# Graph attention with residual norms: running sums in place, keys and values per half of the heads, and a new order of the fill-in work

## The chip, the cores and the metric

The kernel runs on one core of one Trainium2 chip. The metric is the device time of one execution in microseconds (us), the median of several runs. Five engines of the core work side by side, each on its own list of instructions: TensorE (PE in the profile; its weight loads are listed as PEld) multiplies matrices into PSUM, VectorE (DVE) and ScalarE (ACT) compute on SBUF and PSUM, GpSimd (POOL) computes on SBUF, and SyncE (SP) starts DMA transfers. GpSimd starts those DMAs that add to their destination. An engine takes its instructions in the order in which the program gave them to it.

## The reference: what is computed

Eight graphs of 2048 nodes with 256 channels share one adjacency matrix. One layer of masked attention with 8 heads of 32 channels is followed by two normalisations and a small MLP, and the result is added to the input and normalised once more. Cut to what matters:

```python
# x: (8, 2048, 256) float32, adj: (2048, 2048) int32
q, k, v = split(einsum('fnc,ck->fnk', x, w_qkv), 3)         # 8 heads of 32
scores = einsum('fnhd,fmhd->fhnm', q, k) / sqrt(32)
scores = where(adj > 0, scores, -1e9)
t = einsum('fhnm,fmhd->fnhd', softmax(scores), v)
y = layernorm(x + t) * ln1_g + ln1_b
h = relu(y @ w1 + b1)
z = layernorm(y + h @ w2 + b2) * ln2_g + ln2_b
out = layernorm(x + z)
```

## The kernel before

For each graph `f` the nodes are cut into 4 query chunks of 512 (`qc`) and 16 key blocks of 128 (`mb`), and the heads into 2 halves of four (`g`). One **item** is (f, qc, g, mb); there are 8 x 4 x 2 x 16 = 1024 of them, and 16 consecutive items with the same (f, qc, g) are called a **group** here, so a graph is 8 groups. The main loop makes one item after the other:

```python
def scores(item):                       # PE: 4 matmuls, DVE: 2 adds of the mask, ACT: 1 exp
    pt = PT[item] = pp.tile([P, 4, CH], F32, name="p")
    ps2 = [score_pair() for _ in range(2)]          # 2 of 3 pairs of PSUM banks
    for half in (1, 0):
        for j in range(2):
            r = D * (2 * half + j)
            nc.tensor.matmul(ps2[half][:, j, :], KT[f, mb // TPC][r:r + D, g, ...], QT[f, qc][r:r + D, g, :], ...)
    for half, ps in enumerate(ps2):
        nc.vector.tensor_tensor(pt[:, 2 * half:2 * half + 2, :], ps, MK[f, qc][:, mb, None, :]..., ALU.add)
    nc.scalar.activation(pt, pt, AF.Exp, scale=1.0 / math.sqrt(D))

def values(item):                       # PE: 4 matmuls into the group's output bank
    for h in range(4):
        nc.tensor.matmul(O[grp][r:r + D, :], V[f, mb // TPC][:, mb % TPC, ...], PT[item][:, h, :], ...)

def add_up(item):                       # sums of the 16 exp tiles, for the denominators
    for chain in CHAINS:                # ((2, 5, 8, 11), (3, 6, 10, 13)): a DMA adds to the first one
        if mb in chain[1:]:
            nc.gpsimd.dma_start(PT[f, qc, g, chain[0]], PT.pop(item), accum_op=ALU.add)
    if mb == POOLED[1]:                 # POOLED = (0, 1, 4, 7, 9, 12, 14): GpSimd adds into "acc"
        ACC[grp] = ap.tile([P, 4, CH], F32, name="acc")
        nc.gpsimd.tensor_tensor(ACC[grp], PT.pop((f, qc, g, POOLED[0])), PT.pop(item), ALU.add)
    elif mb in POOLED[2:]:
        nc.gpsimd.tensor_tensor(ACC[grp], ACC[grp], PT.pop(item), ALU.add)
```

All other work is cut into steps by generators. A `yield n` means "go on no sooner than n items from now". One bank of PSUM is left for this fill-in work while a group runs; `bank()` hands it out. The generators are `denominator` (per group: 16 matmuls of the sums with ones, then 4 transposes), `tail` (per query chunk: everything after the attention), `project` (per chunk of 512 nodes: queries, keys and values of the next graph), and in the first graph `turn_mask` (the transposed mask, kept in DRAM for the later graphs).

```python
def project(f, c):
    xc = ld.tile(...); nc.sync.dma_start(xc, x[f, c * CH:(c + 1) * CH, :]...)
    yield 3
    while state["turned"]: yield 0
    state["turned"] = True              # one tile "turned" for project and tail
    for a in range(2):                  # 4 transposes, a copy by ACT; yield 1
        ...
    for store, pool, name, k0 in ((KT, kp, "kT", C), (QT, qp, "qT", 0)):
        for g in range(2):              # 2 matmuls of 512 columns, a copy by ACT; yield 1
            ...
    for jj in range(0, TPC, 2):         # V: 4 matmuls of 256 columns, a copy by ACT; yield 1
        for j in range(jj, jj + 2):
            for a in range(2):
                nc.tensor.matmul(ps[...], xT[:, a, j * P:(j + 1) * P], wqkv[:, a, 2 * C:], ...)
    V[f, c] = dst; state["turned"] = False; yield 1

def tail(f, qc):
    while state["y"]: yield 0           # the tail of the chunk before must have ended
    state["y"] = True
    # 2 x (4 transposes, DVE multiplies by 1/denominator); yield 1 each
    nc.gpsimd.dma_start(y, xin, accum_op=ALU.add)       # y += x
    yield 4
    yield from norm(y)                  # DVE statistics of 4 tiles; yield 1; POOL; yield 2; ACT; yield 1
    # 2 x 4 transposes (into "turned"), 2 x 2 matmuls with w1, 2 x 4 matmuls with w2, each with a yield 1
    yield from norm(z)
    nc.gpsimd.dma_start(z, xin, accum_op=ALU.add)       # z += x
    yield 5
    yield from norm(z)
    nc.sync.dma_start(out[...], z); state["y"] = False
```

The main loop (`advance` runs one step of the first generator in the list that is due; `denominator` and `tail` are put at the head of the list):

```python
for t, (f, qc, g, mb) in enumerate(items):
    # ... group starts: load_mask, mask_ahead ...
    if f + 1 < F and qc == NCK - 1:     # the next graph's projections: in the last two groups
        if g == 0 and mb == 0: start(t, projections(f + 1, 0, 1))
        if g == 1 and mb % TPC == 0 and mb: start(t, projections(f + 1, mb // TPC, mb // TPC + 1))
    if mb:
        advance(t)
        if mb % 2: advance(t)
    if t + LEAD < len(items):           # LEAD = 2
        while (nf, nmb // TPC) not in V:            # not projected yet: do it now
            advance(t0); t0 += 1
        scores(items[t + LEAD])
    values(items[t])
    add_up(items[t])
    if mb == LAST: start(t + SUM, denominator(f, qc, g), urgent=True)      # SUM = 4
```

`KT`, `QT` and `V` have 5 tiles each: four chunks of one graph and one more. Before the loop, the constants are loaded by DMAs that SyncE starts, and the first graph is projected.

Of the kernel before, what the change touches and what calls it, by code (L numbers as in the profile page):

```python
# [10 lines left out]
F32 = mybir.dt.float32  # L11
# [16 lines left out]
SUM_MAX = 1e19  # L28

# [23 lines left out]
def fast_path(ctx, tc, cst, x, adj, out, RS):  # L53
# [7 lines left out]
    kp = ctx.enter_context(tc.tile_pool(name="kp", bufs=NCK + 1))  # L61
    qp = ctx.enter_context(tc.tile_pool(name="qp", bufs=NCK + 1))
    vp = ctx.enter_context(tc.tile_pool(name="vp", bufs=NCK + 1))
    pp = ctx.enter_context(tc.tile_pool(name="pp", bufs=9))
    ap = ctx.enter_context(tc.tile_pool(name="ap", bufs=1))
# [11 lines left out]
    state = {"pair": 0, "side": None, "turn": 0, "turned": False, "y": False}  # L77
# [20 lines left out]
    def turn_mask(qc, mc):  # L98
        if mc == 0:
            MK[0, qc] = mkp.tile([P, MB, CH], F8, name="mask")  # L100
        cv = ld.tile([P, TPC, CH], BF16, name="in")
        for half in range(2):
            t = ld.tile([P, 2, CH], I32, name="in")
            q0 = qc * CH + half * 2 * P
            nc.sync.dma_start(t, adj[q0:q0 + 2 * P, mc * CH:(mc + 1) * CH].rearrange("(j p) m -> p j m", p=P))
            nc.vector.tensor_scalar(cv[:, 2 * half:2 * half + 2, :], t, 0.0, MASKED, op0=ALU.is_le, op1=ALU.mult)
            yield 1
        yield 1
        for half in range(2):
            ps = bank(BF16)  # L110
            for r in range(2):
                for j in range(TPC):
                    rr = 2 * half + r
                    nc.tensor.transpose(ps[:, r, j * P:(j + 1) * P], cv[:, j, rr * P:(rr + 1) * P], identb)
            nc.scalar.copy(MK[0, qc][:, mc * TPC + 2 * half:mc * TPC + 2 * half + 2, :], ps, saturate=False)
            yield 1
        if mc == NCK - 1:
            nc.sync.dma_start(MD[qc], MK[0, qc])
# [8 lines left out]
    def project(f, c):  # L127
        xc = ld.tile([P, TPC, C], F32, name="in")
        nc.sync.dma_start(xc, x[f, c * CH:(c + 1) * CH, :].rearrange("(j p) c -> p j c", p=P))
        yield 3  # L130
        while state["turned"]:
            yield 0
        state["turned"] = True
        xT = work.tile([P, 2, CH], F32, name="turned")
        for a in range(2):
            ps = bank()
            for j in range(TPC):
                nc.tensor.transpose(ps[:, j * P:(j + 1) * P], xc[:, j, a * P:(a + 1) * P], ident)
            nc.scalar.copy(xT[:, a, :], ps)
            yield 1  # L140
        for store, pool, name, k0 in ((KT, kp, "kT", C), (QT, qp, "qT", 0)):
            dst = pool.tile([P, 2, CH], F32, name=name)
            for g in range(2):
                ps = bank()
                for a in range(2):
                    nc.tensor.matmul(ps, wqkv[:, a, k0 + g * P:k0 + (g + 1) * P], xT[:, a, :],  # L146
                                     start=(a == 0), stop=(a == 1))
                nc.scalar.copy(dst[:, g, :], ps)  # L148
                if g == 0:
                    yield 1  # L150
            store[f, c] = dst
            yield 1
        dst = vp.tile([P, TPC, C], F32, name="v")
        for jj in range(0, TPC, 2):
            ps = bank()
            for j in range(jj, jj + 2):
                for a in range(2):
                    nc.tensor.matmul(ps[:, (j - jj) * C:(j - jj + 1) * C], xT[:, a, j * P:(j + 1) * P],  # L158
                                     wqkv[:, a, 2 * C:], start=(a == 0), stop=(a == 1))
            nc.scalar.copy(dst[:, jj:jj + 2, :], ps.rearrange("p (b c) -> p b c", c=C))  # L160
            if jj == 0:
                yield 1
        V[f, c] = dst
        state["turned"] = False
        yield 1


    PT, O, OT, DT, ACC, RC = {}, {}, {}, {}, {}, {}

    def scores(item):  # L170
        f, qc, g, mb = item
        pt = PT[item] = pp.tile([P, 4, CH], F32, name="p")
        ps2 = [score_pair() for _ in range(2)]

        for half in (1, 0):
            for j in range(2):
                r = D * (2 * half + j)
                nc.tensor.matmul(ps2[half][:, j, :], KT[f, mb // TPC][r:r + D, g, (mb % TPC) * P:(mb % TPC + 1) * P],  # L178
                                 QT[f, qc][r:r + D, g, :], start=True, stop=True)
        for half, ps in enumerate(ps2):  # L180
            nc.vector.tensor_tensor(pt[:, 2 * half:2 * half + 2, :], ps,  # L181
                                    MK[f, qc][:, mb, None, :].to_broadcast([P, 2, CH]), ALU.add)
        nc.scalar.activation(pt, pt, AF.Exp, scale=1.0 / math.sqrt(D))  # L183
# [3 lines left out]
    def values(item):  # L187
        f, qc, g, mb = item
        grp = (f, qc, g)
        if mb == 0:  # L190
            i = state["side"]
            O[grp] = ps_x[i].tile([P, CH], F32, name=f"x{i}")
        for h in range(4):
            r = D * h
            nc.tensor.matmul(O[grp][r:r + D, :], V[f, mb // TPC][:, mb % TPC, g * P + r:g * P + r + D], PT[item][:, h, :],  # L195
                             start=(mb == 0), stop=(mb == LAST))
        if mb == LAST:
            OT[grp] = op.tile([P, CH], F32, name=f"oT{g}")
            nc.scalar.copy(OT[grp], O.pop(grp))
# [3 lines left out]
    POOLED = (0, 1, 4, 7, 9, 12, 14)  # L203
    CHAINS = ((2, 5, 8, 11), (3, 6, 10, 13))
    SUM = 4

    def add_up(item):
        f, qc, g, mb = item
        grp = (f, qc, g)
        for chain in CHAINS:  # L210
            if mb in chain[1:]:
                nc.gpsimd.dma_start(PT[f, qc, g, chain[0]], PT.pop(item), accum_op=ALU.add)  # L212
        if mb == POOLED[1]:
            ACC[grp] = ap.tile([P, 4, CH], F32, name="acc")
            nc.gpsimd.tensor_tensor(ACC[grp], PT.pop((f, qc, g, POOLED[0])), PT.pop(item), ALU.add)  # L215
        elif mb in POOLED[2:]:
            nc.gpsimd.tensor_tensor(ACC[grp], ACC[grp], PT.pop(item), ALU.add)  # L217


    def norm(t):  # L220
# [5 lines left out]
        yield 1  # L226
# [14 lines left out]
    def denominator(f, qc, g):  # L241
        grp = (f, qc, g)
        terms = [PT.pop((f, qc, g, LAST))] + [PT.pop((f, qc, g, chain[0])) for chain in CHAINS] + [ACC.pop(grp)]
# [7 lines left out]
        yield 1  # L251
        ps = bank()
# [12 lines left out]
    def tail(f, qc):  # L265
        while state["y"]:
            yield 0
        state["y"] = True
# [3 lines left out]
        for gg in range(2):  # L272
            oT = OT.pop((f, qc, gg))
            ps = bank()
# [5 lines left out]
            yield 1  # L280
        nc.gpsimd.dma_start(y, xin, accum_op=ALU.add)
        yield 4
        yield from norm(y)
        while state["turned"]:
            yield 0
        state["turned"] = True
        yT = work.tile([P, 2, CH], F32, name="turned")
        for a in range(2):
            ps = bank()
# [3 lines left out]
            yield 1  # L293
# [3 lines left out]
        for d in range(2):  # L297
            ps = bank()
# [3 lines left out]
            yield 1  # L302
        state["turned"] = False
        z = y
        for jj in range(0, TPC, 2):
            ps = bank()
# [5 lines left out]
            yield 1  # L312
# [4 lines left out]
        yield 5  # L317
        yield from norm(z)
        nc.sync.dma_start(out[f, qc * CH:(qc + 1) * CH, :].rearrange("(j p) c -> p j c", p=P), z)
        state["y"] = False  # L320
# [4 lines left out]
    def start(t, gen, urgent=False):  # L325
        fill.insert(0 if urgent else len(fill), [t, gen])

    def run(e, t):
        wait = next(e[1], None)
        if wait is None:  # L330
            fill.remove(e)
        else:
            e[0] = t + wait
        return wait != 0

    def advance(t):
        for e in list(fill):
            if e[0] <= t and run(e, t):
                return
# [5 lines left out]
    def projections(f, c0, c1):  # L345
        for c in range(c0, c1):
            yield from project(f, c)

    items = [(f, qc, g, mb) for f in range(F) for qc in range(NCK) for g in range(2) for mb in range(MB)]
    LEAD = 2  # L350
    for c in range(NCK):
# [7 lines left out]
    for t, (f, qc, g, mb) in enumerate(items):  # L359
# [6 lines left out]
        if f + 1 < F and qc == NCK - 1:  # L366
            if g == 0 and mb == 0:
                start(t, projections(f + 1, 0, 1))
            if g == 1 and mb % TPC == 0 and mb:
                start(t, projections(f + 1, mb // TPC, mb // TPC + 1))  # L370
        if mb:
            advance(t)
            if mb % 2:
                advance(t)
        if t + LEAD < len(items):
            nf, _, _, nmb = items[t + LEAD]
            t0 = t
            while (nf, nmb // TPC) not in V:
                advance(t0)
                t0 += 1  # L380
# [6 lines left out]
    while fill:  # L387
        t += 1
        advance(t)
# [125 lines left out]
def kernel(  # L515
# [23 lines left out]
    def weight(name, src):  # L539
        t = cst[name] = const.tile([P, 2, src.shape[1]], F32, name=name)  # L540
        nc.sync.dma_start(t, src.rearrange("(a p) k -> p a k", p=P))

    def row_of(pool, name, v):
        t = cst[name] = pool.tile([P, C], F32, name=name)
        nc.sync.dma_start(t, bass.AP(tensor=v.tensor, offset=v.offset, ap=[[0, P], [1, C]]))

    def cols_of(name, v):
        t = cst[name] = const.tile([P, 2], F32, name=name)
        nc.sync.dma_start(t, v.rearrange("(a p) -> p a", p=P))
# [76 lines left out]
```

## Time and profile before

| | value |
|---|---|
| median of 3 runs | 4095.39 us (4093.89 to 4095.95) |
| span of the profiled execution | 4091.3 us |
| first item's mask add starts at | 70.8 us |
| last item's mask add starts at | 4009.6 us |
| mean granted TensorE clock | 0.947 |
| VectorE, ScalarE, GpSimd busy | 67%, 60%, 64% of the span |
| DMA: queue of GpSimd, queue of SyncE | 53.4%, 6.6% of 16 engines' span |

In the profile a line such as `L181 DVE TENSOR_TENSOR p<-s,mask ... x2048 | 2410.5, 1219 | 968.3 <-PE s L178 827.2` reads: source line 181, on VectorE, writes a tile p from s and mask, 2048 times; together 2410.5 us busy, 1219 ns each; the engine stood idle for 968.3 us just before these instructions, 827.2 us of it until the matmuls of line 178 had written s. In the timeline a line begins with the start and the length of a run of equal instructions, and the bracket at its end tells how long the engine had been idle and what ended that. The table of stretches gives, for each stretch of the span, its length, then the busy time of each engine with the number of instructions, the mean granted clock and the share of the DMA engines.

The number of items per group is always 16, so 16 times the shortest distance between items is what a group could take; the distances themselves are read from the starts of the mask adds of line 181, two for each item.

### The profile page before, as it was taken

The numbers are of one execution on the slowest core, as the hardware profiler recorded it, in microseconds if no ns is written. First come the engines' busy times: TensorE is split into PE (matmuls) and PEld (weight loads), VectorE is DVE, ScalarE is ACT, GpSimd is POOL, SyncE is SP. The second block draws the span as 40 slices with busy tenths as digits, with TensorE's granted clock in tenths as the row PEclk, the third lists the DMA queues.
The fourth block names the chain that finished last, engine by engine and source line by source line (L and its number), as shares of the span: only waits on it lengthen the run. The fifth ranks groups of instructions, "written<-read, shape, count | busy, mean of one in ns | idle before, by whom it ended". The sixth has DMA issues, their size and how long they took to land. (4 is left out here: it accounts for less than half of the span.)

```text
span 4091.3 us, 52692 instructions
## 1 busy us (share of the span) xinstructions
PE 3308.0 (81%) x21508; PEld 1011.5 (25%) x21508; DVE 2745.5 (67%) x3175; ACT 2443.2 (60%) x1953; POOL 2624.4 (64%) x1355
## 2 busy tenths in 40 slices
PE   7777788878887888888878878877888878888883
PEld 3222132212222222222222222222222222222221
DVE  3777756777567774777647776477755777567772
ACT  4565555666566664666647666466655666556662
POOL 1576655776567774777747776477754777557774
PEclk9899899999999999999999999999999999999996
DMA  4766745666556664567746667376654677546663
GB/s 122 160 139 150 175 97 105 137 134 147 109 108 144 144 138 99 109 134 152 153 94 130 127 132 150 83 150 145 131 115 99 136 148 157 110 101 135 134 130 74
DMA packets 138792, 525.52 MB, mean 128 GB/s; under 512 B 10160, under 2 KB 76848, under 8 KB 85296
## 3 DMA queue, kind: packets, MB, share of 16 engines
q0 software_dynamic: 89088, 436.24, 53.4%
q1 hardware_dynamic: 49456, 85.86, 6.6%
q8 instruction: 170, 2.79, 0.3%
q14 instruction: 78, 0.64, 0.0%
HBM read 98.44 MB, written 20.97 MB: 29 GB/s over the span
## 5 line engine op out<-in xcount | busy, mean ns | idle before, releaser
L181 DVE TENSOR_TENSOR p<-s,mask 128x1024 f32<-128x1024 f32 x2048 | 2410.5, 1219 | 968.3 <-PE s L178 827.2
L183 ACT ACTIVATE p<-p 128x2048 f32<-128x2048 f32 x1024 | 1951.4, 1910 | 1326.1 <-DVE p L181 1135.6
L217 POOL TENSOR_TENSOR acc<-acc,p 128x2048 f32<-128x2048 f32 x320 | 1505.2, 4704 | 201.5 <-ACT p L183 196.8
L178 PE MATMUL s<-qT,kT 32*128 32x512 f32 x8192 | 1230.3, 671 | 472.9 <-DVE p L181 472.9
L195 PE MATMUL x<-p,v 128*32 128x512 f32 x8192 | 1140.1, 630 | 28.7 <-ACT p L183 28.4
L215 POOL TENSOR_TENSOR acc<-p 128x2048 f32<-128x2048 f32 x64 | 290.9, 4546 | 655.0 <-ACT p L183 508.0
L178 PEld LDWEIGHTS s<-qT,kT 32*128 32x128 f32 x8192 | 333.8, 191 | 1175.7 <-DVE p L181 1077.8
L212 POOL DMA_DIRECT2D p<-p x384 | 362.9, 977 | 362.9 <-ACT p L183 166.3
L195 PEld LDWEIGHTS x<-p,v 128*32 128x32 f32 x8192 | 163.9, 110 | 857.3 <-issue 480.1
L146 PE MATMUL x<-turned,wqkv 128*128 128x512 f32 x480 | 249.2, 645 | 50.9 <-ACT kT L148 29.0
L224 DVE BATCH_NORM_STATS2 st<-y 128x6 f32<-128x256 f32 x384 | 153.9, 401 | 144.3 <-DMA y<-in_x_dram 144.3
L235 ACT ACTIVATE y<-y,nb,rs 128x256 f32<-128x256 f32 x384 | 198.3, 588 | 62.1 <-POOL nb L232 62.1
L248 PE MATMUL x<-p,ones 128*32 128x512 f32 x1536 | 183.1, 610 | 15.8 <-ACT qT L148 14.8
L146 PEld LDWEIGHTS x<-turned,wqkv 128*128 128x128 f32 x480 | 85.4, 197 | 221.1 <-issue 79.8
L158 PE MATMUL x<-wqkv,turned 128*128 128x256 f32 x448 | 112.9, 395 | 31.1 <-ACT v L160 10.1
L300 PE MATMUL x<-turned,w1s 128*128 128x512 f32 x256 | 128.8, 626 | 3.3 <-ACT turned L292 1.0
L309 PE MATMUL x<-w2s,hT 128*128 128x256 f32 x512 | 127.6, 392 | 3.9 <-ACT hT L301 1.3
L228 POOL TENSOR_SCALAR rs<-mv 128x4 f32<-128x4 f32 x96 | 18.4, 191 | 147.9 <-DVE mv L225 144.2
L309 PEld LDWEIGHTS x<-w2s,hT 128*128 128x128 f32 x512 | 92.0, 189 | 69.1 <-ACT hT L301 31.1
L229 POOL TENSOR_TENSOR rs<-rs,mhalf 128x4 f32<-128x4 f32 x96 | 99.5, 1036 | 8.0
L158 PEld LDWEIGHTS x<-wqkv,turned 128*128 128x128 f32 x448 | 81.6, 192 | 77.3 <-ACT qT L148 28.5
L291 PE MATMUL x<-ident,y 128*128 128x128 f32 x256 | 44.6, 294 | 66.9 <-ACT turned L292 46.4
(70 smaller groups left out, 1550.0 us busy)
## 6 DMA issues: line engine op xcount, KB each, us to landing
p<-p POOLq DMA_DIRECT2D x384, 1024.0 KB, 9.3
y<-in_x_dram POOLq DMA_DIRECT2D x64, 512.0 KB, 7.2
mask<-md SPq DMA_DIRECT2D x28, 1024.0 KB, 15.4
in<-in_x_dram SPq DMA_DIRECT2D x32, 512.0 KB, 21.7
in<-in_adj_dram SPq DMA_DIRECT2D x32, 512.0 KB, 5.9
out_dram<-y SPq DMA_DIRECT2D x32, 512.0 KB, 8.3
md<-mask SPq DMA_DIRECT2D x4, 1024.0 KB, 12.7
wqkv<-in_L_gnn_w_qkv_dram SPq DMA_DIRECT2D x1, 768.0 KB, 4.6
```

Of the source, the lines that this page charges most:

```text
L146: nc.tensor.matmul(ps, wqkv[:, a, k0 + g * P:k0 + (g + 1) * P], xT[:, a, :], start=(a == 0), stop=(a == 1))
L158: nc.tensor.matmul(ps[:, (j - jj) * C:(j - jj + 1) * C], xT[:, a, j * P:(j + 1) * P], wqkv[:, a, 2 * C:], start=(a == 0), stop=(a == 1))
L178: nc.tensor.matmul(ps2[half][:, j, :], KT[f, mb // TPC][r:r + D, g, (mb % TPC) * P:(mb % TPC + 1) * P], QT[f, qc][r:r + D, g, :], start=Tr ...
L181: nc.vector.tensor_tensor(pt[:, 2 * half:2 * half + 2, :], ps, MK[f, qc][:, mb, None, :].to_broadcast([P, 2, CH]), ALU.add)
L183: nc.scalar.activation(pt, pt, AF.Exp, scale=1.0 / math.sqrt(D))
L195: nc.tensor.matmul(O[grp][r:r + D, :], V[f, mb // TPC][:, mb % TPC, g * P + r:g * P + r + D], PT[item][:, h, :], start=(mb == 0), stop=(mb ...
L212: nc.gpsimd.dma_start(PT[f, qc, g, chain[0]], PT.pop(item), accum_op=ALU.add)
L215: nc.gpsimd.tensor_tensor(ACC[grp], PT.pop((f, qc, g, POOLED[0])), PT.pop(item), ALU.add)
L217: nc.gpsimd.tensor_tensor(ACC[grp], ACC[grp], PT.pop(item), ALU.add)
L235: nc.scalar.activation(t[:, j, :], t[:, j, :], AF.Identity, bias=nb[:, j:j + 1], scale=rs[:, j:j + 1])
L248: nc.tensor.matmul(ps[r:r + D, :], cst["ones"], term[:, h, :], start=(n == 0), stop=(n == 3))
L309: nc.tensor.matmul(ps[:, (j - jj) * C:(j - jj + 1) * C], hT[:, d, j * P:(j + 1) * P], w2s[:, d, :], start=(d == 0), stop=(d == 1))
```

## The change: what it does

- **Running sums in the tile of their first block.** The tile `acc` is gone: GpSimd adds to the exp tile of block 0 in place. The blocks that it adds are now (0, 3, 5, 8, 10, 12, 14), and the DMA chains begin with blocks 1 and 2. The pool of exp tiles has 10 tiles where it had 9.
- **Keys and values per half of the heads.** Instead of one tile for both halves there is one for each, so a half is free again when its group is done. The values are now computed 128 columns at a time.
- **Fill-in work that asks for the bank.** A generator yields `BANK` when its next step needs the one spare bank, and `TURNED` when it needs the tile of that name. One call of `advance` goes through all generators that are due and hands out one bank (two at odd items in the last group of a graph and the first half of the next one's first group). Steps without a bank are not limited. The flag `y` is gone, so that two tails may be under way, and the waits after the two adding DMAs are 5 and 7 items for 4 and 5. The statistics of `norm` are split over two items.
- **The next graph over five groups.** The four projections of the next graph start in groups 5, 7 and 8 (two of them) of the current one, and the last may reach into the next graph's first group.
- **Constants** are loaded by DMAs that ScalarE starts.

```diff
-    kp = ctx.enter_context(tc.tile_pool(name="kp", bufs=NCK + 1))
+    kp = ctx.enter_context(tc.tile_pool(name="kp", bufs=2 * NCK + 2))
-    vp = ctx.enter_context(tc.tile_pool(name="vp", bufs=NCK + 1))
-    pp = ctx.enter_context(tc.tile_pool(name="pp", bufs=9))
-    ap = ctx.enter_context(tc.tile_pool(name="ap", bufs=1))
+    vp = ctx.enter_context(tc.tile_pool(name="vp", bufs=2 * NCK + 2))
+    pp = ctx.enter_context(tc.tile_pool(name="pp", bufs=10))
...
     def project(f, c):
-        while state["turned"]:
-            yield 0
+        yield TURNED
         state["turned"] = True
...
-        dst = vp.tile([P, TPC, C], F32, name="v")
-        for jj in range(0, TPC, 2):
+        for g in range(2):
+            yield BANK
+            v = vp.tile([P, TPC, P], F32, name="v")
             ps = bank()
-            for j in range(jj, jj + 2):
+            for j in range(TPC):
                 for a in range(2):
-                    nc.tensor.matmul(ps[:, (j - jj) * C:(j - jj + 1) * C], xT[:, a, j * P:(j + 1) * P],
-                                     wqkv[:, a, 2 * C:], start=(a == 0), stop=(a == 1))
+                    nc.tensor.matmul(ps[:, j * P:(j + 1) * P], xT[:, a, j * P:(j + 1) * P],
+                                     wqkv[:, a, 2 * C + g * P:2 * C + (g + 1) * P], start=(a == 0), stop=(a == 1))
...
-    POOLED = (0, 1, 4, 7, 9, 12, 14)
-    CHAINS = ((2, 5, 8, 11), (3, 6, 10, 13))
+    POOLED = (0, 3, 5, 8, 10, 12, 14)
+    MOVED = ((1, 4, 7, 11), (2, 6, 9, 13))
...
-        if mb == POOLED[1]:
-            ACC[grp] = ap.tile([P, 4, CH], F32, name="acc")
-            nc.gpsimd.tensor_tensor(ACC[grp], PT.pop((f, qc, g, POOLED[0])), PT.pop(item), ALU.add)
-        elif mb in POOLED[2:]:
-            nc.gpsimd.tensor_tensor(ACC[grp], ACC[grp], PT.pop(item), ALU.add)
+        if mb in POOLED[1:]:
+            first = PT[f, qc, g, POOLED[0]]
+            nc.gpsimd.tensor_tensor(first, first, PT.pop(item), ALU.add)
...
     def norm(t):
...
-        yield 1
+            if j % 2:
+                yield 1
...
     def tail(f, qc):
-        while state["y"]:
-            yield 0
-        state["y"] = True
...
         nc.gpsimd.dma_start(y, xin, accum_op=ALU.add)
-        yield 4
+        yield 5
...
         nc.gpsimd.dma_start(z, xin, accum_op=ALU.add)
-        yield 5
+        yield 7
...
-    def advance(t):
+    def advance(t, banks):
         for e in list(fill):
-            if e[0] <= t and run(e, t):
-                return
+            while e[0] <= t:
+                if e[2] == BANK:
+                    if not banks:
+                        break
+                    banks -= 1
+                elif e[2] == TURNED and state["turned"]:
+                    break
+                e[2] = next(e[1], None)
+                if e[2] is None:
+                    fill.remove(e)
+                    break
+                if e[2] > 0:
+                    e[0] = t + e[2]
...
+    AHEAD = [(NCK - 2, 0, MB // 2), (NCK - 1, 0, MB // 2), (NCK - 1, 1, 0), (NCK - 1, 1, MB // 2)]
...
-        if f + 1 < F and qc == NCK - 1:
-            if g == 0 and mb == 0:
-                start(t, projections(f + 1, 0, 1))
-            if g == 1 and mb % TPC == 0 and mb:
-                start(t, projections(f + 1, mb // TPC, mb // TPC + 1))
+        if f + 1 < F and (qc, g, mb) in AHEAD:
+            start(t, project(f + 1, AHEAD.index((qc, g, mb))))
         if mb:
-            advance(t)
-            if mb % 2:
-                advance(t)
+            hurry = (g, qc) == (1, NCK - 1) or (f and g == qc == 0 and mb < MB // 2)
+            advance(t, 2 if hurry and mb % 2 else 1)
...
     def weight(name, src):
-        nc.sync.dma_start(t, src.rearrange("(a p) k -> p a k", p=P))
+        nc.scalar.dma_start(t, src.rearrange("(a p) k -> p a k", p=P))
```

## The prediction

> **What bounds the kernel now.** I read the page first, then the starts of the mask adds (two for each item), the table of stretches for the fourth graph, and the timeline where items stood far apart.
>
> ```profile
> PE 3308.0 (81%) x21508; PEld 1011.5 (25%) x21508; DVE 2745.5 (67%) x3175; ACT 2443.2 (60%) x1953; POOL 2624.4 (64%) x1355
> L181 DVE TENSOR_TENSOR p<-s,mask 128x1024 f32<-128x1024 f32 x2048 | 2410.5, 1219 | 968.3 <-PE s L178 827.2
> L217 POOL TENSOR_TENSOR acc<-acc,p 128x2048 f32<-128x2048 f32 x320 | 1505.2, 4704 | 201.5 <-ACT p L183 196.8
> ```
>
> No engine is full. The first and third lines would suggest PE or POOL; the second tells more: the mask adds, which pace an item with nothing else in it, waited 968 us. A quiet item takes 2.55 us (mask adds start at 1749.82 and 1752.38): 2.36 of DVE and a gap. PE needs 2.06 for the same item (matmuls of line 178 start at 2006.96, those of 195 at 2008.03, the next work at 2009.02), so fill-in work beyond 0.49 us in an item lengthens it. 1024 x 2.55 is 2611 us; 4095 is paid.
>
> ```profile
> core 0: us, PE busy (x) PEld busy (x) DVE busy (x) ACT busy (x) POOL busy (x), PEclk, DMA share, GB/s
> 1554.20:1652.30 98.10, 78.34 (x412) 28.17 (x408) 43.44 (x53) 46.73 (x48) 40.91 (x25) 0.97 0.40 85
> 1652.30:1705.80 53.50, 46.67 (x328) 14.04 (x324) 41.26 (x45) 35.95 (x26) 38.51 (x19) 1.00 0.58 119
> 1705.80:1752.40 46.60, 39.29 (x304) 9.81 (x302) 40.87 (x46) 35.08 (x27) 38.45 (x19) 1.00 0.65 138
> 1752.40:1817.40 65.00, 50.64 (x328) 14.74 (x324) 43.26 (x53) 35.98 (x26) 44.73 (x25) 0.89 0.69 140
> 1817.40:1865.50 48.10, 40.79 (x304) 10.07 (x302) 40.87 (x46) 35.10 (x27) 39.42 (x19) 0.96 0.64 139
> 1865.50:1930.00 64.50, 50.84 (x328) 14.74 (x324) 43.26 (x53) 35.98 (x27) 42.57 (x24) 0.89 0.69 142
> 1930.00:1984.30 54.30, 49.32 (x328) 13.61 (x324) 40.84 (x45) 38.95 (x32) 40.17 (x21) 0.97 0.68 147
> 1984.30:2048.00 63.70, 55.21 (x356) 18.83 (x352) 43.29 (x54) 37.65 (x33) 43.63 (x23) 0.97 0.68 146
> ```
>
> The eight groups of one graph, 493.8 us together. The first is twice as long as the third with the same 16 items; the fourth and sixth have about 18 us more than the groups before them. Graphs two to seven repeat this within 2 us. So there are two holes.
>
> **Hole one, forced projections.** In the first group three distances are 20.8, 17.6 and 16.1 us. The program needs keys that are not there yet and pushes the projection in at one place:
>
> ```profile
> 1566.28 2.35 DVE L181 TENSOR_TENSOR p<-s,mask 128x1024 f32<-128x1024 f32 x2 [3.17 <-PE s L178]
> ...
> 1580.41 0.58 ACT L160 COPY v<-x 128x512 f32<-128x512 f32 x1 [3.26 <-PE x L158]
> ...
> 1587.06 2.36 DVE L181 TENSOR_TENSOR p<-s,mask 128x1024 f32<-128x1024 f32 x2 [3.19 <-PE s L178]
> ```
>
> ACT's copies wait for PE and PE's next bank for the copy, because one bank is spare, and nothing hides it.
>
> **Hole two, a DMA in DVE's way.** In the fourth group the first distance is 10.9 us:
>
> ```profile
> 1743.98 2.28 POOL L281 DMA_DIRECT2D y<-in_x_dram  x1
> ...
> 1761.11 0.43 DVE L224 BATCH_NORM_STATS2 st<-y 128x6 f32<-128x256 f32 x1 [6.37 <-DMA y<-in_x_dram]
> ...
> 1764.54 2.09 PE L178 MATMUL s<-qT,kT 32*128 32x512 f32 x8 [8.75 <-DVE p L181]
> ```
>
> DVE stands before the statistics until y has landed, 17 us after its issue, while ready scores lie behind. The page's median for this DMA is 7.2 us; here a mask load of 1 MB and an output store were issued at 1740.3 to 1740.8. The list of waits has 144.3 us of it in 25 cases.
>
> [...] after 8.75 us idle the score matmuls took 2.09 us, against 1.14 elsewhere[...] in the trace SP spends 0.74 to 7.35 us on eleven constants before it issues the first x.
>
> **The change part by part**, for a middle graph.
>
> Base: four query chunks without either hole. First groups (46.6 + 48.1) / 2 = 47.4. Second groups 65.0 and 64.5, less the excess of their first items (10.9 and 10.2 against 2.5): 56.7. Together 104.1, times 4: **416**. The eighth group loses 2.6 in the same way, so waits make 8.4 + 7.7 + 2.6 = 19, and the projections the rest: 493.8 - 416 - 19 = **59**.
>
> Projections after. Spare tiles now come free during group 7, so I count no forced burst: walking the yields with one bank an item (two where the text allows it), chunk 1 ends early in group 8, chunk 2 at its item 13, chunk 3 at item 7 of the next graph's first group, before item 10 asks for it. A chunk has 2 banks of transposes (0.6 us: 2.06 + 0.6 - 2.55 = 0.1 over a quiet item), 4 of queries and keys (1.93, so 1.45 over) and 2 of values. The values lose: 8 matmul instructions of 256 columns took 1.97 us, and there will be 16 of 128. Transposes of 128 columns stand 0.147 us apart (4 in 0.59), a 128-column weight load of line 158 lasts 0.192; I take 0.165 as an estimate between them: 2.64 us, 2.1 over. One chunk is 0.2 + 5.8 + 4.2 = 10.2 us, four are 41. About nine items take two banks; each saves 0.49 of slack less and waits for a copy. Such waits are 0.88 (2027.03, for DVE) and 1.57 us (2013.32, for ACT) in the timeline: 1.2 as a mean, with the lost slack about 1.6 x 9 = 14. That makes 55; some 5 us of statistics fall into these items, where DVE has room. **50**, so 9 less than before.
>
> Waits after. The y DMA is now issued at item 7 of the first group, away from the mask load, and read five items (some 13 us) later. Ahead of it lies one 1 MB adding DMA (median 9.3 us), then its own half megabyte, 4 to 5 us: it lands about when it is wanted. I leave 4 of 19 us: **15 less**. The z DMA gets seven items.
>
> In sum 24 us a graph, 144 for six. The last graph (479.3) has no next one: its 43 us of projections shrink to chunk 3, about 16, and its waits of some 20 to 5: 42. The first (494.5) mostly makes masks and now carries three projections where it had little more than one: gain 5. At the end, DVE waits at 4022.6 for the tail before the last (4.99 us idle, 2.1 us of its statistics) ahead of the last one's work; without the flag y about 8 come back. At the start the constants no longer delay x (6 us), but eight value banks cost 0.7 more each: nothing. Total 144 + 42 + 5 + 8 = 199, so 4095 - 199 = **3896, say 3900**.
>
> In place sums: 6 adds of 4.7 us a group as before. POOL's wait for the old acc (147.0 us behind line 248, in the list of waits) goes, but POOL wasn't on the path: DVE never waited for it. I count nothing.
>
> **Rivals.** (1) POOL becomes the bound: it is busy 38.5 us in a group of 46.6; were all groups that fast, the tail's POOL work would leave little, and ten tiles with three held (nine with two before) leave the same seven for rotation. For it: 4.7 us adds and DMAs in one order. Against: groups will average about 59, with 41 of POOL. It would cost up to 60: 3960. (2) The holes merely move: banks in pairs stall as the bursts did, or y lands late because the adding DMAs stand ahead on one queue. That keeps two thirds of the loss: 4000. (3) The spread work hides better than I allow, value banks cost little and both holes close: projections 42 and no waits, 13 more a graph: 3800.
>
> **Range and chances.** Third rival and second set the ends, drawn in a little above: 3800 to 3985. The holes are seen in every graph and the text treats both, so under 4013 (2% less) is likely, 0.90; within 2% 0.08; slower 0.02, for a group that waits for exp tiles or a projection that still comes late.
>
> **What would show it.** First groups of graphs two to eight near 55 to 65 us with no distance over 9; second groups near 57 and the wait of the statistics for y under 50 us in all; value matmuls x16 a bank at about 2.6 us; mask adds' idle time down from 968 to about 770; POOL's 147 us wait gone. I am wrong if mask adds wait for POOL or an adding DMA, if a distance of 15 us remains in a first group, or if second groups stay at 65.

## The result, and the profile after

The changed kernel takes **4039.34 us** (median of 4 runs, 4035.44 to 4056.27) against 4095.67 for the kernel before, run beside it: a ratio of **0.9868, 95% interval [0.9839, 0.9898]**. It is faster by 56 us. I had predicted 3900 us and a range that ends at 3985: the prediction is wrong, by 139 us. To a result within 2% of the time before, as this one is, I had given a chance of 0.08.

From the page of the changed kernel: the busy times, then the mask adds, the running sums, now `p<-p`, and the statistics (busy time and mean ns of one, then the idle time ahead of the group and what ended it).

```profile
PE 3291.4 (82%) x22020; PEld 1044.4 (26%) x22020; DVE 2732.3 (68%) x3175; ACT 2440.2 (60%) x1953; POOL 2621.6 (65%) x1355
L179 DVE TENSOR_TENSOR p<-s,mask 128x1024 f32<-128x1024 f32 x2048 | 2410.4, 1219 | 1083.8 <-PE s L176 902.5
L212 POOL TENSOR_TENSOR p<-p 128x2048 f32<-128x2048 f32 x384 | 1790.3, 4663 | 931.2 <-ACT p L181 912.3
L219 DVE BATCH_NORM_STATS2 st<-y 128x6 f32<-128x256 f32 x384 | 155.9, 406 | 23.3 <-DMA y<-in_x_dram 23.3
```

The last line answers to hole two: DVE stood 144.3 us before the statistics, now 23.3, both cases outside the middle graphs. Yet the second line has more idle time, not less: 1083.8 us against 968.3, and 902.5 of it ends with PE's scores. DVE's waits for y have shrunk by 121 us, and those of the mask adds for PE's scores have grown by 75.

The table of stretches of the changed kernel says where. Its rows are the first, second, fourth and eighth group of the fourth graph (stretch, its length, each engine's busy time with instruction counts, granted clock, DMA share, GB/s).

```profile
1569.00:1635.60 66.60, 54.43 (x356) 17.32 (x352) 43.17 (x54) 39.28 (x35) 37.22 (x21) 0.95 0.51 106
1635.60:1693.20 57.60, 48.38 (x328) 14.47 (x324) 41.17 (x46) 36.44 (x28) 38.96 (x21) 0.97 0.59 123
...
1741.60:1799.30 57.70, 49.10 (x328) 14.16 (x324) 41.22 (x46) 36.09 (x27) 40.51 (x23) 0.97 0.66 143
...
1970.20:2053.40 83.20, 69.61 (x428) 27.48 (x424) 41.36 (x45) 40.65 (x38) 40.19 (x19) 0.98 0.48 112
```

The first group fell from 98.1 to 66.6 us, the fourth from 65.0 to 57.7. The eighth rose from 63.7 to 83.2: 428 matmul records instead of 356. The program takes two banks in every second item there. The timeline of the changed kernel shows one such item (start, duration, engine, line, operation, out<-in, idle time before it and what ended it):

```profile
1979.07 1.98 PE L150 MATMUL x<-turned,wqkv 128*128 128x512 f32 x4 [1.47 <-ACT oT L197]
...
1980.98 2.06 ACT L231 ACTIVATE y<-y,nb,rs 128x256 f32<-128x256 f32 x4
1982.95 0.56 ACT L152 COPY qT<-x 128x512 f32<-128x512 f32 x1
1983.56 2.05 PE L159 MATMUL x<-wqkv,turned 128*128 128x128 f32 x16 [2.51 <-ACT qT L152]
...
1986.82 2.35 DVE L179 TENSOR_TENSOR p<-s,mask 128x1024 f32<-128x1024 f32 x2 [7.74 <-PE s L176]
```

The first bank is done at 1981.05. ACT gets to its copy at 1982.95, for an exp and the tail's normalisation lie ahead in its order. PE waits 2.51 us for that copy, and the scores of the next item lie behind the second bank. DVE waits 7.74 us; from mask add to mask add it is 10.09.

### The profile page after: what moved, and what is told of

The parts are those of the page before. It is cut to its first block, busy times and chain, and to the rows that moved or that the text cites. A ratio compares the mean times of both kernels' runs of the same rounds, so it can differ in the third digit from the quotient of the medians.

```text
span 4037.3 us, 53723 instructions
## 1 busy us (share of the span) xinstructions
PE 3291.4 (82%) x22020; PEld 1044.4 (26%) x22020; DVE 2732.3 (68%) x3175; ACT 2440.2 (60%) x1953; POOL 2621.6 (65%) x1355
## 3 DMA queue, kind: packets, MB, share of 16 engines
q10 hardware_dynamic: 2352, 1.97, 0.2%
## 5 line engine op out<-in xcount | busy, mean ns | idle before, releaser
L179 DVE TENSOR_TENSOR p<-s,mask 128x1024 f32<-128x1024 f32 x2048 | 2410.4, 1219 | 1083.8 <-PE s L176 902.5
L212 POOL TENSOR_TENSOR p<-p 128x2048 f32<-128x2048 f32 x384 | 1790.3, 4663 | 931.2 <-ACT p L181 912.3
L176 PE MATMUL s<-qT,kT 32*128 32x512 f32 x8192 | 1212.2, 662 | 354.4 <-DVE p L179 353.5
L193 PE MATMUL x<-p,v 128*32 128x512 f32 x8192 | 1118.1, 618 | 21.4 <-ACT p L181 21.2
L150 PE MATMUL x<-turned,wqkv 128*128 128x512 f32 x480 | 244.5, 634 | 75.9 <-ACT kT L152 44.2
L245 PE MATMUL x<-p,ones 128*32 128x512 f32 x2048 | 236.3, 602 | 18.9 <-DMA p<-p 8.9
L219 DVE BATCH_NORM_STATS2 st<-y 128x6 f32<-128x256 f32 x384 | 155.9, 406 | 23.3 <-DMA y<-in_x_dram 23.3
L159 PE MATMUL x<-wqkv,turned 128*128 128x128 f32 x896 | 124.9, 297 | 34.1 <-ACT qT L152 20.2
L312 POOL TENSOR_TENSOR y<-y,g2r 128x1024 f32<-128x1024 f32 x32 | 78.1, 2442 | 101.8 <-ACT y L231 101.8
L159 PEld LDWEIGHTS x<-wqkv,turned 128*128 128x128 f32 x896 | 113.5, 206 | 77.2 <-ACT qT L152 38.6
L290 POOL TENSOR_TENSOR y<-y,g1r 128x1024 f32<-128x1024 f32 x32 | 75.7, 2367 | 60.0 <-issue 57.3
L245 PEld LDWEIGHTS x<-p,ones 128*32 128x32 f32 x2048 | 64.0, 111 | 186.2 <-issue 137.2
L287 PE MATMUL x<-ident,y 128*128 128x128 f32 x256 | 53.9, 318 | 62.5 <-ACT y L231 24.4
```

What stands on the lines that cost most here:

```text
L159: nc.tensor.matmul(ps[:, j * P:(j + 1) * P], xT[:, a, j * P:(j + 1) * P], wqkv[:, a, 2 * C + g * P:2 * C + (g + 1) * P], start=(a == 0), s ...
L176: nc.tensor.matmul(ps2[half][:, j, :], KT[f, mb // TPC, g][r:r + D, (mb % TPC) * P:(mb % TPC + 1) * P], QT[f, qc][r:r + D, g, :], start=Tr ...
L193: nc.tensor.matmul(O[grp][r:r + D, :], V[f, mb // TPC, g][:, mb % TPC, r:r + D], PT[item][:, h, :], start=(mb == 0), stop=(mb == LAST))
L212: nc.gpsimd.tensor_tensor(first, first, PT.pop(item), ALU.add)
L219: nc.vector.bn_stats(st, t[:, j, :])
L245: nc.tensor.matmul(ps[r:r + D, :], cst["ones"], term[:, h, :], start=(n == 0), stop=(n == 3))
```

## The experiments

All kernels here compute the whole reference. The kernel before took 4097 to 4099 us beside them. Letters in the quoted expectations are names for explanations as they came up; I say in words which one is meant. In line numbers of the changed kernel, 138 to 161 are the projection and its copies, 176 the scores, 179 the mask adds, 181 exp, 209 and 212 the sums.

**Two banks an item, or one.** The rule for haste is dropped; a bank is given once an item everywhere.

```diff
-            advance(t, 2 if hurry and mb % 2 else 1)
+            advance(t, 1)
```

> The changed kernel with one bank for each item everywhere, never two. Then the last two chunks come late and some six of their banks are pushed in at one place in the next graph's first group. Theory A (pairs are dear): eighth group down by 15 us or more, first group up by as much or less; 4000 to 4050 us. Rival C (the second bank is what closes the hole): the first group goes back to over 90 us and nothing is gained in the eighth; about 4180 us.

3868.48 us, 0.9447 [0.9428, 0.9465]: **171 us less than the change as written.** The eighth group of the fourth graph takes 62.5 us instead of 83.2; that graph 464.2 instead of 484.4. The mean of the six middle graphs falls from 486 to 464, the first graph from 524.4 to 501.1, the last by 4, the stretch after the last mask add by 12: 6 x 22 + 23 + 4 + 12 = 171. I had expected a gain of at most 40 us. No forced burst comes back (the longest distance in the first group of a middle graph is 5.77 us), so the haste bought nothing.

**The opposite dose.** Two banks in every second item of every group.

```diff
-            advance(t, 2 if hurry and mb % 2 else 1)
+            advance(t, 2 if mb % 2 else 1)
```

> The changed kernel with two banks at every odd item instead of in nine items a graph. Theory A (the second bank of an item waits for ScalarE's copy of the first): the loss grows with the number of pairs; some five to eight pairs more a graph, most of them with a small second bank, 10 us or more a graph: 4110 us or more. Rival L (it is where the banks lie that made the difference, not their pairing): 4040 us within 20.

4635.81 us, 1.1323 [1.1292, 1.1354]. The direction is right, the size no clean measure of pairs: PE also waited 200 us for the x of projections (12 cases), against 7.3 us in one case in the change.

**Whose copy is it?** PE waits for ACT's copy of a bank. If ACT's order is what makes it late, the same copy on DVE should shorten the wait, though DVE paces the items.

```diff
-            nc.scalar.copy(xT[:, a, :], ps)
+            nc.vector.tensor_copy(xT[:, a, :], ps)
```

and the same for the copies of keys, queries and values.

> The changed kernel with the eight copies of a projection chunk on VectorE in place of ScalarE. Theory A (two banks in one item are dear because the second waits for ScalarE's copy of the first, and that copy stands behind an exp which waits for VectorE): the wait of PE for the copy shrinks from 2 to 3.4 us to under 1, the eighth group falls from 84.8 us to about 72, the first from 66.6 to about 60; 20 us a graph, in all about 3900 us. Rival B (the pairs cost what TensorE's work costs, and VectorE paces the items): 256 copies of 0.6 us more on VectorE; 4040 to 4140 us.

3919.52 us, 0.9569 [0.9549, 0.9589], 120 us less than the change: with pairs left in, a graph takes 466 instead of 486. PE's waits for the copies of keys, 44.2 us in the change, the longest 3.4, are now:

```profile
PE x L150 <- DVE kT L152: 17.9, 20, 1.2
```

In the preparation ahead of the first group this is worse (first mask add at 81.4 us instead of 68.4), so later kernels use DVE only from the first group on.

> One bank for each item, and in the main loop the copies of the projections on VectorE. Theory A (PE's waits for a copy that stands behind an exp are what remains of the loss): PE's waits for copies of turned, kT, qT and v fall from about 100 us to 20, and 3868 us becomes about 3830. Rival B (with one bank an item ScalarE's copy is in time, and VectorE has no room): 3870 to 3900 us.

One bank and DVE's copies: 3789.89 us, 0.9255 [0.9239, 0.9271]. That is 79 less than one bank alone. So single banks too had waited for ACT's order.

The four kernels also say how much of a pair's cost is ACT's order. Going from pairs to single banks takes 21.7 us off a middle graph when ACT copies (485.8 to 464.1) and still 14.6 when DVE copies (466.0 to 451.4). So ACT's order is about a third of the cost. The other two thirds stay with the pair whoever copies; no run separates what they consist of.

**The same for the tail**, where ACT evacuates four banks with a scale and bias:

```diff
-nc.scalar.activation(yT[:, a, :], ps, AF.Identity, bias=..., scale=...)
+nc.vector.tensor_scalar(yT[:, a, :], ps, cst["g1c"][:, a:a + 1], cst["be1c"][:, a:a + 1], op0=ALU.mult, op1=ALU.add)
-nc.scalar.activation(hT[:, d, :], ps, AF.Relu, bias=..., scale=1.0)
+nc.vector.tensor_scalar(hT[:, d, :], ps, cst["b1s"][:, d:d + 1], 0.0, op0=ALU.add, op1=ALU.max)
```

> One bank for each item, copies of the projections on VectorE, and the four evacuations of a tail (transposed y, hidden layer) on VectorE too. Theory A (each copy that leaves ScalarE's queue takes a wait of TensorE with it; about 80 us of such waits remain): 3790 us becomes about 3755. Rival B (VectorE is full enough): 3790 us or more.

**3740.1 us, 0.9129 [0.91, 0.9158]: the fastest kernel here, and below both figures of the expectation.** DVE's lists of waits agree (who <- whom: us in all, cases, longest). From the list of the kernel with one bank alone:

```profile
DVE p L179 <- PE s L176: 712.9, 489, 9.4
```

From that of one bank with the projection's copies on DVE:

```profile
DVE p L179 <- PE s L176: 514.4, 498, 9.6
```

From that of the fastest, with the tail's copies on DVE too:

```profile
DVE p L179 <- PE s L176: 352.8, 451, 9.5
```

The change had 902.5 in this place. DVE took on work (2732.3 us busy in the change, 2959.4 in the last kernel) and the wait that set the pace fell by 550 us.

**The in-place sums.** First undone beside one bank: an `acc` tile, nine `p` tiles and the old lists of blocks.

```diff
+                ACC[grp] = ap.tile([P, 4, CH], F32, name="acc")
+                nc.gpsimd.tensor_tensor(ACC[grp], PT.pop((f, qc, g, POOLED[0])), PT.pop(item), ALU.add)
-            first = PT[f, qc, g, POOLED[0]]
-            nc.gpsimd.tensor_tensor(first, first, PT.pop(item), ALU.add)
```

> One bank for each item, and the running sums as before the change: a tile acc, 9 exp tiles, the old block lists. Theory H (GpSimd wasn't on the path, as predicted): 3868 us within 15. Rival I (the wait of GpSimd for the old acc delays the tail's small operations and the adding DMAs, now that groups are faster): 3890 to 3930 us.

3944.75 us, 0.9623 [0.9607, 0.9639], so the in-place sums are worth **76 us** there, with the tenth exp tile and the new lists of blocks, which no run separates from them. The lists of waits of this kernel (`acc` and `p` are the running sum and the exp tiles) show what comes back:

```profile
POOL acc L214 <- PE x L249: 469.9, 33, 28.1
...
DVE p L180 <- DMA p<-p: 102.5, 46, 5.9
```

POOL stands for the single `acc` until PE has read the last group's sums, 28 us at most. The adding DMAs, issued by POOL, stand behind it in its order and go late: in the mean 4.8 us after the end of the exp that made their tile, against 2.9 with in-place sums (one bank). DVE waits for exp tiles that they still hold; with in-place sums that second wait is 29.3 us.

Then done alone, in the kernel before:

> The kernel before with the in-place sums alone (first block's tile, new block lists, 10 exp tiles). Theory H (the sums are worth something only where groups are fast, 76 us beside the other parts, little here): 4070 to 4095 us. Rival I (the old acc held things up in every group of the kernel before too): 4020 us or less, which would leave the rest of the change with a loss.

4028.06 us, 0.9831 [0.9804, 0.9857]: **71 us of gain from this part alone**, and the interval overlaps the whole change's. It lies between the two expectations, nearer to the rival's. As written, with pairs, everything else in the change together brought nothing that can be told from zero. Half of hole two went with it:

```profile
DVE st L221 <- DMA y<-in_x_dram: 68.3, 21, 15.5
```

144.3 us before, 68.3 here, 23.3 in the change. The y DMA is issued in its old place and lands 12.4 us after issue in the median, against 16.9 before and 10.3 in the change. The forced bursts of the first group are all still there (distances 19.1, 15.9, 16.0).

**The waits of 5 and 7 items.** Put nearer to the old 4 and 5:

```diff
-        yield 5
+        yield 4
-        yield 7
+        yield 5
```

> The changed kernel with the waits after the two adding DMAs of a tail back at 4 and 5 items (they are 5 and 7). Theory F (the DMA lands about when it is wanted, and each item of wait counts): VectorE waits 2 to 3 us for y in most of the 24 tails, second groups 2 to 4 us longer; about 4090 us. Rival G (the DMA is early because no mask load lies beside it any more): no change or a little less, 4030 to 4045 us.

4177.81 us, 1.0194 [1.0168, 1.022], 138 slower than the change and slower than the kernel before. But not for y and z as I had it: the statistics' wait for y is 38.2 us. The timeline of this kernel (SPq is SyncE's queue of issues):

```profile
1880.53 0.38 SPq L317 DMA_DIRECT2D out_dram<-y  x1
1880.96 2.10 SPq L129 DMA_DIRECT2D in<-in_x_dram  x1
...
1906.36 1.12 PE L138 MATMUL x<-ident,in 128*128 128x128 f32 x4 [20.87 <-DMA in<-in_x_dram]
```

With these waits the output store precedes the next projection's x in SyncE's order. The store waits for the tail, x waits for the store, and PE, which reached the projection in its own order, for x: 117.6 us in six cases. With 5 and 7 the same x was issued at 1732.88 in the change: 164 us after its graph began, where it is 270 here. Two kernels tested that. The first issues x from ACT:

```diff
-        nc.sync.dma_start(xc, ...)
+        nc.scalar.dma_start(xc, ...)
```

> The changed kernel with waits of 4 and 5 items (as in the run that took 4178 us), and the x of a projection loaded by a DMA that ScalarE starts. Theory J (with the shorter waits the output store stands ahead of the x load in SyncE's queue and holds it until the last normalisation is done, so TensorE waits 20 us for x six times): the 117.6 us wait for x goes, about 4050 us. Rival F (the shorter waits themselves cost): stays at 4150 to 4180 us.

4201.06 us, 1.0253 [1.0232, 1.0273], and it settles nothing: in ACT's order x stood behind the normalisation, so it was issued at 1896.14, 265 us after its graph began and hardly sooner, and PE waited until 26.6 us after the issue, with a store and a mask under way. The start, where x now stands behind ACT's constants, grew by 18 us. The second leaves SyncE and asks four items earlier, ahead of the store:

```diff
+            if f + 1 < F and (qc, g, mb + 4) in AHEAD:
+                ask_x(f + 1, AHEAD.index((qc, g, mb + 4)))
```

> The changed kernel with waits of 4 and 5 items, and each projection's x asked for four items earlier, ahead of the output store in SyncE's queue. Theory J (4178 us came from x behind the store, not from the waits themselves): TensorE's 117.6 us wait for x goes, 4040 to 4070 us. Rival F (the shorter waits cost by themselves): 4150 us or more.

4055.2 us, 0.9892 [0.9862, 0.9921]: 123 of 138 us come back, and the fifth group returns from 72.8 to 52.0 us. The order in SyncE's queue is the cause of nearly all of it.

**Two misses, on the first graph**, which grew from 494.5 to 524.4 us. Its masks are turned there, now one bank an item. Giving back the extra wait after each mask bank:

```diff
             nc.scalar.copy(...)   # mask
+            yield 1
```

> The changed kernel with a yield 1 after each of the two banks of a mask chunk, as before the change. Theory D (the first graph is 30 us slower than before because the next adjacency tile is asked for one item before it is used, so VectorE waits for its DMA): first graph back from 524 us to about 495, VectorE's wait for the adjacency from 65.8 to about 40 us; about 4010 us. Rival E (the first graph is slower because it now carries three projections): no change, 4039 us.

4034.86 us, 0.9851 [0.9829, 0.9872]; the first graph 521.0. No gain worth the name; but DVE's wait for the adjacency, which this should have cut to 40 us, only went from 65.8 to 58.2. Then the adjacency's halves asked for two items or more ahead of use, on the kernel with one bank and DVE's copies:

```diff
+        t = ask(qc, mc, 1)
+        yield 2
         nc.vector.tensor_scalar(cv[:, 2:4, :], t, 0.0, MASKED, op0=ALU.is_le, op1=ALU.mult)
```

> As the run with one bank and copies on VectorE, and in the first graph each half of an adjacency tile is asked for when the half before it has been turned to bf16, two items or more before its use. Theory K (VectorE's wait for the adjacency, 67 us in the run with one bank, is what is left of the first graph's loss): that wait falls under 20 us and the first graph from 501 to about 465 us; 35 us less than the run with copies on VectorE. Rival E (it is the projections): no change.

3792.12 us, 0.9264 [0.9248, 0.9279], as without it. Within the first graph DVE's wait for the adjacency fell from 37.9 to 8.6 us, and yet the graph did not shrink (500.6 against 494.7). The reason is in the timeline of this kernel (line 223 is the running sum, 114 DVE's conversion of the adjacency to bf16):

```profile
89.79 4.54 POOL L223 TENSOR_TENSOR p<-p 128x2048 f32<-128x2048 f32 x1 [3.90 <-ACT p L192]
91.12 3.76 DVE L114 TENSOR_SCALAR in<-in 128x1024 bf16<-128x1024 int32 x1
```

The conversion takes 0.69 us where no GpSimd add runs. Here it begins during one and ends 0.55 us after it. In this kernel 19 of the graph's 24 conversions are longer than that, and together they take 71.7 us instead of 35.0. In the change's trace the seven conversions longer than 0.7 us (1.70 to 4.84) ended 0.54 to 0.56 us after the GpSimd operation in which they began. What the wait gave back, the conversions took. So the explanation was not tested cleanly and stays open.

## Why the prediction was wrong, point by point

Against my sum, the six middle graphs take 485.8 us each in the mean, 8.4 less than before and not 24 (94 in all), the first 35 more than predicted, the last 6 more (443 for 437), the end 13 more, the start 2 less. That is 146, against 143 between 3896 and 4039.

- **Forced bursts, right.** Distances of 16 to 21 us are gone; the first group of a middle graph takes 66.6 us, just over the 55 to 65 I named, and its longest distance is 8.46.
- **Waits for y, right in size, half wrong in cause.** 23.3 us are left where I allowed 50, and the second group of the fourth graph takes 57.6. I gave it all to the later read and the distance from the mask load. With the old place kept, the in-place sums alone took away 76 of 144. And a landing after 17 us was no exception: the page's 7.2 us is the median over y and z together, and y alone had 16.9. The 4 to 5 us for y's own half megabyte were an estimate, about half of the 9.3 us that 1 MB had; z of the same size took 6.3.
- **"About nine items take two banks ... 1.6 x 9 = 14": the step that failed.** Pairs cost 22 us in a middle graph, 23 in the first, and 171 in all, where the sum had 14 in each of six graphs, 84. These 87 us are the largest part of what is missing. The term of the wait was too small: I took 1.2 us from two single waits, one of them for DVE. In a pair, ACT's copy stands behind an exp, an `oT` copy or a normalisation of 2.06 us, and PE waits 2.0 to 3.4. From PE's list of waits of the change, the three that contain them:

```profile
PE x L138 <- ACT turned L139: 50.0, 20, 3.6
PE x L150 <- ACT kT L152: 44.2, 20, 3.4
PE x L159 <- ACT qT L152: 20.2, 13, 2.5
```

The means are 2.5, 2.2 and 1.6 us. That is ACT's order, about 7 of the 22 us; with DVE's copies pairs still cost 14.6, by chance what I had put down for all of it. Second and wider: I took the other banks at PE's excess alone, the time over a quiet item. With one bank an item, moving the copies to DVE still took 79 us off, so that sum also lacked ACT's order.
- **The base of 416 was low as well.** Groups 3 and 4 of a middle graph carry no projection. In the change they take 48.6 and 58.1 us in the mean, and four such pairs are 427, as an estimate, where base and waits made 420. That leaves 59 us for the projections, where I had 50.
- **Value banks at 2.64 us: too high.** Sixteen matmul instructions of 128 columns took 2.05 us, 1.98 from the first to the start of the next work, as eight of 256 had (1.97). That is 0.124 us each, although one weight load lasts 0.192: the 16 loads of a bank took 1.86 us in all, beside the matmuls. My 0.165 was an estimate between the 0.147 of the transposes and the 0.192 of one load. This gave back some 5 us a graph of what pairs lost.
- **"In place sums ... I count nothing": wrong.** Alone 71 us, beside one bank 76. I asked only whether DVE waited for POOL by name. The lists show the wait passed on through DMAs: POOL's wait delays the issue of adding DMAs (4.8 us after the exp for 2.9), DVE waits for exp tiles that they hold (102.5 us for 29.3), and y lands later (16.9 us for 12.4). Some of POOL's 147.0 us was on the path after all, under another name. The 71 us do not come on top of my sum: part of them are the waits for y, which I had counted under another cause.
- **First graph, 5 us less predicted, 30 more measured.** Pairs account for 23 of it. Against the in-place sums alone, which bring this graph to 484.2, the loss is even 40. DVE's wait for the adjacency grew from 8.5 to 38.4 us in it; the two kernels that were to remove this wait left most of it or lengthened the conversions in its place. So the rest stays open, and part of it may be that the graph carries three projections.
- **The end, 8 us less predicted, 5 more measured** (81.7 to 87.0 us after the last mask add). The timeline of the change:

```profile
3958.03 1.41 POOL L209 DMA_DIRECT2D p<-p  x1
...
3968.58 3.64 PE L245 MATMUL x<-p,ones 128*32 128x512 f32 x16 [8.91 <-DMA p<-p]
```

The last denominators wait 8.9 us for an adding DMA that POOL issued only at 3958.03, after the tail's own work in its order. I had gone by DVE's waits alone. With one bank an item POOL's last add and this DMA come ahead of the tail's work, PE waits 1.1 us there, and the stretch is 75.1: the 6.6 us less than before are close to the 8 of the prediction. So the pairs took them away.

- **The start.** I said nothing would change; it is 2.4 us shorter (first mask add 70.8 to 68.4). x lands at 7.3 us, but ACT makes its first copy at 12.29, after the constants that it now issues and a table load of 1.28 us:

```profile
7.32 1.94 PE L138 MATMUL s<-ident,in 128*128 128x128 f32 x8 [7.32 <-DMA in<-in_x_dram]
11.00 1.28 ACT L139 ACT_TABLE_LOAD   x1 [11.00 <-DMA g1r<-in_L_gnn_ln_g_dram]
12.29 1.07 ACT L139 COPY turned<-s 128x512 f32<-128x512 f32 x2
```

**The rivals.** POOL as the bound fell: in the fastest kernel it is busy 2620.7 of 3736.9 us. "The holes merely move: banks in pairs stall as the bursts did" was the right one, with 4000 us the nearest of my figures; its other half, y landing late, did not come (23.3 us of waits). The third rival, well-hidden banks at 3800, is near what one bank with DVE's copies gives (3790), though by copies that the change does not contain: that nearness is luck.

## What to carry to other kernels

Where one PSUM bank is spare, each piece of fill-in work waits for whoever empties the bank (here PE for ACT's copies of keys 44.2 us, up to 3.4 at a time). Count the place of that copy in its engine's order, not only the matmuls. Try it on the engine whose order reaches it soonest, even a busier one (128 us here, in two steps), and do not ask for two banks in one item (171 us here). An engine that nobody waits for by name may still issue DMAs: its waits reach the path under the names of those transfers (71 and 76 us here). When a wait in items is changed, see which DMA issues change places in a queue (123 of 138 us here). And when a wait is gone and the time is not, see whether the instruction behind it grew longer (conversions of 71.7 us in all for 35.0 here).

## What the runs showed of the hardware, unexpected

- Float matmuls of 128 columns with fresh 128-column weights took 0.124 us each (1.98 us from the first of 16 to the next work), half of the 0.240 of those with 256 columns (1.92 us from the first of 8 to the next work, at 1583.93 of the trace before). Each weight load was recorded as 0.19 us; the 16 of a bank took 1.86 us in all, beside the matmuls.
- A y transfer of half a megabyte landed 16.9, 12.4 and 10.3 us after issue (medians: before, in-place sums alone, change); the z transfer of the same size took 6.3 before and 6.4 in the change. That the adding DMAs ahead of it make the difference fits, but was not tested by itself.
- DVE's conversion of an adjacency half (128 x 1024, int32 to bf16) took 0.69 us alone and up to 4.84 when it began during a GpSimd add (the change, at 337.50): it ended 0.54 us after the add had.
- DVE took over copies from PSUM and scores still reached its mask adds sooner: 227 us more busy and 550 less waiting, between the change and the fastest kernel (190 of the 550 came with single banks).
